# Four-layer graph network on one core: the neighbour product of layer 1 in seven half-size products, the other whole, and three engines queued by hand up to the first expert

## The chip, the core and the metric

The kernel runs on one core of one Trainium2 chip. A core has a TensorE (PE) for matrix products, a VectorE (DVE), a ScalarE (ACT), a GpSimd (POOL) and a SyncE (SP) whose queue issues most transfers from device memory. Engines run side by side and wait for each other by semaphores. Matrix products are written into PSUM, eight banks of 128 x 512 float32; the other engines take them from there. The metric is the device time of one execution in microseconds (us), the median of several runs.

## The reference

512 nodes, 512 features, 16384 edges (src, dst); four layers, each on a normalised, rectified copy of x and added to x. Cut to layers 1 and 2, around which the change stands:

```python
h = jnp.maximum(_layernorm(x, axis=-1), 0.0)
x = x + _L1_gnn_ref(h, ...)
#   alpha = h @ wc;  beta = h @ wn
#   sums = segment_sum(beta[dst], src);  gamma = sums / counts[:, None]
#   return alpha + gamma + bias
h = jnp.maximum(_layernorm(x, axis=-1), 0.0)
x = x + _L2_gnn_ref(h, ...)
#   gates = softmax(h @ gate_W + gate_b), the two largest of four experts
#   each expert, twice: h = relu(aggr(h) @ W_l + b_l + h @ W_r), aggr the mean over neighbours
```

Layer 0 is an attention layer with a feed-forward part and two norms; layer 3 a graph convolution. The tolerance of the output asks for float32 products; sums over neighbours are done with a matrix of edge counts, exact in the faster reduced form (fp32r), so that only the other factor is split into a high and a low part.

## The kernel before

Nodes are tiled in four blocks of 128 (`xs[:, b, :]`, `h[:, b, :]`), and a product over features needs the transposed copy `hT[:, k, nodes]`, which `turn` (L189) makes: four transposes on PE into one bank, one ScalarE copy out. `mm` (L196) is a row of products into one bank. Weights come by `load_w` (L81) into five rotating buffers, on SP's queue; a load waits until the products that read the buffer's last content are done.

**Layer 0's end.** `ff_down` (L427) gives the feed-forward result of block b; `residual` (L379) adds h on DVE; `norm2_a`, `norm2_b`, `norm2_c` (L433 to L445) are the layer's norm, the addition to xs, and the next layer's norm with rectification. A norm's statistics and small steps are on DVE (L145 to L161, L175), its logarithm and exponential (L138, L140) and final scaling (L182) on ScalarE. Up to the product of block 3 the order of PE, DVE and ScalarE is written out by hand (`tc.manual_schedule`, L480); block 3's norm stands after it (L700, L708).

**Layer 1** (L735 to L781). `beta_of` (L742): one block of hT times wns, four products of 128x512, then `split` (L711) on ScalarE (high part) and DVE (low part). `alpha_of` (L747): a bias add on DVE, one block of hT times wcs, an add on DVE. `gamma_of` (L753): the neighbour sum of a block, eight fp32r products of the count matrix CT with both parts of beta, needing all four blocks of beta; then scaling and addition to xs (L756), layer 2's norm with h and its high part hs (L182, L184) on ScalarE, the low part (L758) on DVE. Only PE's order is by hand here (L760): beta 0, transposes 2, beta 1, alpha 0 and 1, transposes 3, beta 2 and 3, alpha 2 and 3, sums 0 to 2, transposes of layer 2's block 0, sum 3, transposes 1. DVE's and ScalarE's orders are set by the scheduler, from priorities and readiness as it models them.

**Layer 2's start** (L781 to L795): per block the gate products (`pg`) and the sums over neighbours of h (`pag`), transposes of blocks 2 and 3 between them.

**Seven half products.** `seven` (L819) does a 512x512 product with seven instead of eight products of halves (Strassen's scheme in Winograd's form): `left_sums` (L799) and `right_sums` (L809) form four sums of quarters of each factor on DVE, `product` (L824) is one half-size product (eight records of 128x256 in the profile), and `plus` (L832) adds a bank to a tile on DVE. Every expert uses it (`hidden` L887, `outer` L937). In `seven` the products come in the order 0, 5, 4, 6, 1, 3, 2; two sums (u2, u3) read bank b between products 5, 6 and 3, which add to the same bank. `XR` (L865, L869) are the right sums of hT and agT for all experts, `weights0` (L872) loads an expert's two first weights and makes their left sums; both `weights0(0)` and `weights0(1)` stand ahead of `hidden(0)`, and the scheduler has put their sums wherever DVE was free, from the feed-forward part on. `gates` (L899) is a row of small DVE instructions.

Of the kernel before, what the change touches and what calls it, by code (L numbers as in the profile page):

```python
# [18 lines left out]
P = 128  # L19
# [17 lines left out]
def fast(  # L37
# [442 lines left out]
    with tc.manual_schedule(engines={ET.PE, ET.DVE, ET.Activation}):  # L480
# [206 lines left out]
        nc.vector.reciprocal(ideg_b, ideg_b)  # L687
        ff_up(1, 4)
# [11 lines left out]
    y23 = residual(p3, 3, "y2")  # L700
# [7 lines left out]
    norm2_c(3, norm2_b(3, *norm2_a(3, y23)))  # L708
    ffp.release()

    def split(hi, lo, full, copy):  # L711

        copy(hi, full)  # L713
        nc.vector.tensor_sub(lo, full, hi.bitcast(F32))
# [3 lines left out]

    ideg = main.tile([P, NB], F32, name="ideg")
    icnt = main.tile([P, NB], F32, name="icnt")  # L720
    nanf = main.tile([P, NB], F32, name="nanf")
    nc.vector.tensor_scalar(ideg, deg[:, :NB], 1.0, None, op0=ALU.max)
    nc.vector.reciprocal(ideg, ideg)
    isd1 = main.tile([P, NB], F32, name="isd1")
    nc.vector.tensor_scalar(isd1, deg[:, :NB], 1.0, None, op0=ALU.add)
    rs4 = rsqrt_end(*rsqrt_begin(isd1, NB, "isd"))
    isd = main.tile([P, NB], F32, name="isd")
    nc.vector.tensor_copy(isd, rs4)
    nc.vector.tensor_scalar(icnt, cnt, 1.0, None, op0=ALU.max)
    nc.vector.reciprocal(icnt, icnt)  # L730
    nc.vector.reciprocal(nanf, cnt)
    nc.vector.tensor_scalar(nanf, nanf, 0.0, None, op0=ALU.mult)


    wcs, wns = load_w(wc, "wcs"), load_w(wn, "wns")  # L735
    bias1_b = load_bc(bias1, "bias1_b")

    pair = main.tile([P, 2, NB, D], F32, tag="pair", name="pair")
    beta = pair.bitcast(R)
    hs = main.tile([P, 2, NB, D], R, tag="hs", name="hs")  # L740

    def beta_of(b):  # L742
        p = bank(f"pbe{b}")
        mm(p, [(blk(hT, k, b), wns[:, k, :]) for k in range(KB)])
        split(beta[:, 0, b, :], beta[:, 1, b, :], p, nc.scalar.copy)

    def alpha_of(b):  # L747
        nc.vector.tensor_add(xs[:, b, :], xs[:, b, :], bias1_b)
        p = bank(f"pal{b}")
        mm(p, [(blk(hT, k, b), wcs[:, k, :]) for k in range(KB)])  # L750
        nc.vector.tensor_add(xs[:, b, :], p, xs[:, b, :])

    def gamma_of(b):  # L753
        p = bank(f"psu{b}")
        mm(p, [(blk(CT, j, b), beta[:, i, j, :]) for j in range(NB) for i in range(2)])
        nc.vector.scalar_tensor_tensor(xs[:, b, :], p, icnt[:, b:b + 1], xs[:, b, :], op0=ALU.mult, op1=ALU.add)  # L756
        norm_relu((b,), "n2_", hs[:, 0, b, :])
        nc.vector.tensor_sub(hs[:, 1, b, :], h[:, b, :], hs[:, 0, b, :].bitcast(F32))  # L758

    with tc.manual_schedule(engines={ET.PE}):  # L760
        beta_of(0)
        turn(hT, h, 2, "h2_")
        beta_of(1)
        alpha_of(0)
        alpha_of(1)
        turn(hT, h, 3, "h2_")
        beta_of(2)
        beta_of(3)
        alpha_of(2)
        alpha_of(3)  # L770
        for b in range(NB - 1):
            gamma_of(b)
        turn(hT, h, 0, "h3_")
        gamma_of(3)
        turn(hT, h, 1, "h3_")

    ct_p.release()
    te_p = ctx.enter_context(tc.tile_pool(name="te_p", bufs=1, side="right", reuse_waits="tile"))


    pg = bank("pg")  # L781
    pag = [bank(f"pag{k}") for k in range(KB)]
    with tc.manual_schedule(engines={ET.PE}):
        for b in range(NB):
            mm(pg[:, b * NX:(b + 1) * NX], [(blk(hT, k, b), gw[:, k, :]) for k in range(KB)])
            for k in range(KB):
                for i in range(2):
                    nc.tensor.matmul(pag[k], blk(hs[:, i, :, :], b, k), C[:, b, :], start=(b == 0 and i == 0),
                                     stop=(b == NB - 1 and i == 1))
            if b < 2:  # L790
                turn(hT, h, b + 2, "h3_")
# [7 lines left out]
    def left_sums(t, s, keep=None):  # L799

        a11, a12, a21, a22 = (quarter(t, j, i) for i in range(2) for j in range(2))
        nc.vector.tensor_add(s[:, 0], a21, a22)
        nc.vector.tensor_sub(s[:, 1], s[:, 0], a11)
        last = a21 if keep is None else keep
        nc.vector.tensor_sub(last, a11, a21)
        nc.vector.tensor_sub(s[:, 2], a12, s[:, 1])
        return a11, a12, s[:, 2], a22, s[:, 0], s[:, 1], last

    def right_sums(t, s, keep=None):  # L809

        b11, b12, b21, b22 = (quarter(t, i, j) for i in range(2) for j in range(2))
        last = b12 if keep is None else keep
        nc.vector.tensor_sub(s[:, 0], b12, b11)
        nc.vector.tensor_sub(s[:, 1], b22, s[:, 0])
        nc.vector.tensor_sub(last, b22, b12)
        nc.vector.tensor_sub(s[:, 2], b21, s[:, 1])
        return b11, b21, b22, s[:, 2], s[:, 0], s[:, 1], last

    def seven(name, terms, first, result):  # L819


        pa, pb, pc = (bank(f"{name}_{i}").rearrange("p (m n) -> p m n", m=2) for i in "abc")

        def product(p, i, some, fresh=False):  # L824
            for m in range(2):
                for l, r in some:
                    for k in range(2):
                        nc.tensor.matmul(p[:, m, :], l[i][:, k, m * P:(m + 1) * P], r[i][:, k, :], start=fresh,  # L828
                                         stop=(k == 1), skip_group_check=True)
                        fresh = False  # L830

        def plus(x, p, y):  # L832
            t = uu.tile([P, 2, W], F32, tag="u", name=f"u_{name}") if y is None else y
            nc.vector.tensor_add(t, p, x)  # L834
            return t
# [16 lines left out]
    ws = ctx.enter_context(tc.tile_pool(name="ws", bufs=4, reuse_waits="tile"))  # L852
    uu = ctx.enter_context(tc.tile_pool(name="uu", bufs=6, reuse_waits="tile"))

    def sums_tile(name):
        return ws.tile([P, 3, 2, W], F32, tag="ws", name=f"ws_{name}")

    def copied(p):
        t = uu.tile([P, 2, W], F32, tag="u", name="u_first")
        nc.scalar.copy(t, p)  # L860
        return t, t

    pair = main.tile([P, 2, NB, D], F32, tag="pair", name="sums")
    sums = pair.rearrange("p g s (k n) -> p g s k n", k=2)
    XR = [right_sums(hT, sums[:, 0, 0:3], sums[:, 0, 3])]  # L865
    agT = main.tile([P, KB, N], F32, tag="agT", name="agT")
    for k in range(KB):
        nc.vector.tensor_mul(agT[:, k, :], pag[k], ideg_b)
    XR.append(right_sums(agT, sums[:, 1, 0:3], sums[:, 1, 3]))  # L869
    eTs = {}  # L870

    def weights0(e):  # L872
        l = []
        for nm, src_w in (("wr0", Wr), ("wl0", Wl)):
            w = load_w(src_w[e, 0], f"{nm}_{e}")
            l.append(left_sums(w, sums_tile(f"{nm}_{e}")))
        return l
# [603 lines left out]
```

## Time and profile before

| | |
|---|---|
| three runs | 522.4, 521.95, 521.9 us; median 521.95 |
| the profiled execution | 522.04 us, its span 520.4 us, mean granted PE clock 0.986 |
| PE busy | 482.4 us, 93% of the span |
| DVE busy | 356.5 us, 68% |
| ACT busy | 155.8 us, 30% |
| POOL busy | 2.8 us |
| layer 1's first product to expert 0's first product, on PE | from 208.40 to 261.24 us |

Times in the profile are microseconds from the span's start. Each row of a timeline gives the start, the length, the engine, the line of the kernel, the operation, what is written from what, shapes, and how many records are merged; a bracket gives the idle time before and what ended it. A float32 product has two records in the trace, an fp32r one has one. The length of a PE row contains the way through the array, so consecutive rows overlap; the time that a group takes of PE is from its start to the next group's. The chain of work that ended last is followed back from the end: at each step to what released it. A table of stretches gives per stretch the busy time of PE, PE's weight loads, DVE, ACT and POOL with the number of instructions, then the clock granted to PE as a share of full speed.

### The profile page before, as it was taken

How to read it: one execution, taken by the hardware profiler on the slowest of the kernel's cores; microseconds unless marked ns; L12 is line 12 of the kernel's file. 1: busy time of each engine (PE TensorE's matmuls, PEld its weight loads, DVE VectorE, ACT ScalarE, POOL GpSimd, SP SyncE). 2: the span in 40 equal slices, each digit the busy share in tenths (PEclk: the TensorE clock that was granted, in tenths of full speed). 3: DMA queues.
4: the chain of work that ended last, by engine and by line, in shares of the span. 5: the costliest groups of instructions: out<-in, count | busy, mean ns of one | idle time of the engine just before them, and what ended most of it. 6: DMA issues, size and time to landing. Idle time of an engine off the chain costs nothing.

```text
span 520.4 us, 5638 instructions
## 1 busy us (share of the span) xinstructions
PE 482.4 (93%) x2159; PEld 358.9 (69%) x2159; DVE 356.5 (68%) x731; ACT 155.8 (30%) x316; POOL 2.8 (1%) x10
## 2 busy tenths in 40 slices
PE   2999889697999999998999999999999999999993
PEld 1798556354774584445888888888888888885552
DVE  8899999998987776928562547831687136656642
ACT  3886344341531231312402131021202121122452
POOL 2000000000000000000000000000000000000000
PEclk9999999979999999999999999999999999999998
DMA  7810201300002133422002141200322040000002
GB/s 253 296 70 1 81 1 48 115 22 0 1 21 66 55 124 119 142 73 90 0 1 91 71 151 37 102 35 20 144 81 81 1 161 1 0 1 1 0 1 85
DMA packets 18497, 34.41 MB, mean 66 GB/s; under 512 B 1528, under 2 KB 2080, under 8 KB 18464
## 3 DMA queue, kind: packets, MB, share of 16 engines
q1 hardware_dynamic: 17504, 32.47, 18.5%
q10 hardware_dynamic: 960, 1.51, 0.8%
q8 instruction: 19, 0.31, 0.3%
q14 instruction: 14, 0.11, 0.1%
HBM read 32.93 MB, written 1.05 MB: 65 GB/s over the span
## 4 chain that ended last, share of the span: by engine, by line
PE 74%; DVE 18%; ACT 3%; issue 2%; DMA 1%; ACTq 0%; DVEq 0%
PE pe_b L828 8%; PE pff L198 5%; PE pe_a L828 5%; PE pf L430 5%; PE pe_c L828 5%; PE pq L198 5%; PE pz_b L828 3%; PE po_b L828 3%; PE pqk L198 3%; PE pwo L377 3%; PE pbe L198 3%; PE ph L198 3%; PE cps L273 2%; DVE m L304 2%; PE pz_c L828 2%; PE po_a L828 2%
## 5 line engine op out<-in xcount | busy, mean ns | idle before, releaser
L834 DVE TENSOR_TENSOR u_pe<-pe_b,u_first 128x512 f32<-128x512 f32 x12 | 8.3, 692 | 55.7 <-PE pe_b L828 55.7
L198 PE MATMUL pq<-zz,C 128*128 128x512 f32 x128 | 32.7, 409 | 0.0
L271 DVE TENSOR_SCALAR ohs<-iota_h,src_f,dw_i 128x256 bf16<-128x256 f16 x104 | 28.8, 340 | 1.7 <-PE cps L273 1.6
L198 PE MATMUL pff<-hT,w 128*128 128x256 f32 x128 | 28.6, 381 | 0.7 <-issue 0.7
L198 PEld LDWEIGHTS pq<-zz,C 128*128 128x128 f32 x128 | 24.1, 189 | 6.6 <-issue 1.2
L273 PE MATMUL cps<-ohs,ohd 128*128 128x256 bf16 x104 | 19.5, 289 | 9.7 <-DVE ohs L271 9.7
L430 PE MATMUL pf<-w,ffT 128*128 128x512 f32 x64 | 28.1, 592 | 0.0
L932 ACT ACTIVATE re<-te,gt 128x512 f32<-128x512 f32 x16 | 11.6, 723 | 54.8 <-DVE te L930 54.8
L894 ACT ACTIVATE eT<-u_pe,vecs 128x256 f32<-128x256 f32 x24 | 10.9, 500 | 56.5 <-DVE u_pe L834 56.5
L198 PEld LDWEIGHTS pff<-hT,w 128*128 128x128 f32 x128 | 24.1, 190 | 5.0 <-issue 1.7
L273 PEld LDWEIGHTS <-ohd 128*128 128x128 f16 x128 | 15.7, 145 | 13.6 <-DVE ohd L266 8.0
L299 PE MATMUL psc<-qT,kT 64*128 64x256 f32 x128 | 17.8, 421 | 4.2 <-DVE s L310 4.2
L430 PEld LDWEIGHTS pf<-w,ffT 128*128 128x128 f32 x64 | 11.9, 190 | 13.9 <-issue 13.9
L304 DVE TENSOR_REDUCE m<-psc 128x256 f32<-128x2048 f32 x8 | 18.3, 2286 | 1.7 <-PE cps L273 1.2
L310 DVE TENSOR_TENSOR s<-psc,m 128x1024 f32<-128x1024 f32 x16 | 18.8, 1215 | 0.1
L713 ACT CAST zz<-u_pz 128x512 fp32r<-128x512 f32 x12 | 7.4, 618 | 37.7 <-DVE u_pz L834 37.7
L299 PEld LDWEIGHTS psc<-qT,kT 64*128 64x128 f32 x128 | 13.2, 204 | 7.8 <-issue 6.5
L348 PE MATMUL aps<-s,v 128*64 128x256 f32 x128 | 15.8, 388 | 3.0 <-DVE nt_l L145 3.0
L338 DVE TENSOR_TENSOR s<-s,r 128x2048 f32<-128x2048 f32 x8 | 18.3, 2286 | 0.1
L311 ACT ACTIVATE s<-s 128x1024 f32<-128x1024 f32 x16 | 16.8, 1054 | 3.3 <-DVE s L310 2.8
L933 DVE TENSOR_TENSOR xs<-xs,re 128x512 f32<-128x512 f32 x16 | 11.0, 690 | 9.3 <-ACT re L932 9.3
L828 PE MATMUL pe_b<-sums,wr 128*128 128x256 f32 x64 | 16.4, 379 | 0.0
(264 smaller groups left out, 1039.9 us busy)
## 6 DMA issues: line engine op xcount, KB each, us to landing
wr<-in_L_gnn_Wr_dram SPq DMA_DIRECT2D x8, 1024.0 KB
wl<-in_L_gnn_Wl_dram SPq DMA_DIRECT2D x8, 1024.0 KB
w<-in_L_gnn_W_dram SPq DMA_DIRECT2D x5, 1024.0 KB
wk<-in_L_gnn_Wk_dram SPq DMA_DIRECT2D x1, 1024.0 KB
wq<-in_L_gnn_Wq_dram ACTq DMA_DIRECT2D x1, 1024.0 KB
wv<-in_L_gnn_Wv_dram SPq DMA_DIRECT2D x1, 1024.0 KB
wo<-in_L_gnn_Wo_dram SPq DMA_DIRECT2D x1, 1024.0 KB
bl_b<-in_L_gnn_bl_dram SPq DMA_DIRECT2D x4, 256.0 KB
```

Source lines behind the costliest of these rows:

```text
L198: nc.tensor.matmul(p, a, c, start=(i == 0), stop=(i == len(pairs) - 1))
L271: nc.vector.tensor_scalar(ohs, iota_h, src_f[:, c:c + 1], dw_f[:, c:c + 1], op0=ALU.is_equal, op1=ALU.mult)
L273: nc.tensor.matmul(cps, ohd[0][:, :, c % 8], ohs, start=(c == 0), stop=(c == NCH - 1))
L299: nc.tensor.matmul(psc[i][:, 4 * g + j, :], kT[o:o + HD, j, b * P:(b + 1) * P], qT[o:o + HD, j, cols], start=True, stop=True)
L304: nc.vector.tensor_reduce(m, psc[i].rearrange("p h n -> p n h"), axis=AX.X, op=ALU.max)
L310: nc.vector.tensor_sub(s[:, g, :], psc[i][:, g, :], m[:, None, :].to_broadcast([P, 4, W]))
L311: nc.scalar.activation(s[:, g, :], s[:, g, :], AF.Exp, scale=1.0 / 8.0)
L338: nc.vector.tensor_mul(s, s, rz[i].to_broadcast([P, H, W]))
L348: nc.tensor.matmul(aps[hf][j // 2][o:o + HD, j % 2, :], v[:, b, (2 * j + g) * HD:(2 * j + g + 1) * HD], s[:, 4 * g + j, :], start=(b == 0 ...
L377: nc.tensor.matmul(p, blk(qT, k, b), wo[:, k, :], start=(k == 0), stop=(k == KB - 1))
L430: nc.tensor.matmul(p, ffT[b // 2][:, f, c:c + P], w2[f // 4][:, f % 4, :], start=(f == 0), stop=(f == FB - 1))
L828: nc.tensor.matmul(p[:, m, :], l[i][:, k, m * P:(m + 1) * P], r[i][:, k, :], start=fresh, stop=(k == 1), skip_group_check=True)
```

## The change

- beta is no longer made by blocks but by the seven half products, in an order of its own (0, 1, 4, 5, 6, 3, 2); `product` and `plus` become functions of their own, and `left_sums` and `right_sums` are taken apart into steps that can be queued one by one. beta's quarters are split as they come (`split_hi` returns the subtraction to be queued later).
- alpha stays whole, and its blocks stand between beta's products: 0, 1, 2 early, 3 last.
- From the last block of the feed-forward part to the sums of agT, PE, DVE and ScalarE are all in one hand-written order, with block 3's norm, expert 0's left sums (`f0`, taken in the gaps), the gates, the neighbour sums and, at the end, expert 1's left sums (`F1 = weights0(1)`).
- In the neighbour sums, each block's add of the next sum stands between the statistics and the small steps of its norm; the gates of a block stand before the next transposes.
- The small tiles of degrees (ideg, icnt, nanf, isd) are made earlier, after the long reciprocal L687, and their two ScalarE instructions stand ahead of the copies of feed-forward groups 4 and 6. The bias adds of layer 1, which the scheduler had put into layer 0's norms, are queued before alpha's adds.

The order after, from the diff (helpers such as `alpha_mm`, `gamma_mm`, `turn_pe` issue PE's part and return the other engine's):

```diff
+    def product(p, i, some, fresh=False):
+        for m in range(2):
+            for l, r in some:
+                for k in range(2):
+                    nc.tensor.matmul(p[:, m, :], l[i][:, k, m * P:(m + 1) * P], r[i][:, k, :], start=fresh,
+                                     stop=(k == 1), skip_group_check=True)
+                    fresh = False
+    def plus(x, p, y=None):
+        t = uu.tile([P, 2, W], F32, tag="u", name="u_sum") if y is None else y
+        nc.vector.tensor_add(t, p, x)
+        return t
...
+    def beta_quarter(i, j, value):
+        return split_hi(*(beta[:, g, 2 * i:2 * i + 2, j * W:(j + 1) * W] for g in range(2)), value)
+    def gamma_begin(b):
+        return norm_relu_begin((b,), "n2_")
+    def gamma_end(b, begun):
+        norm_relu_end((b,), "n2_", begun, hs[:, 0, b, :])
...
-    with tc.manual_schedule(engines={ET.PE}):
-        beta_of(0)
...
+    with tc.manual_schedule(engines={ET.PE, ET.DVE, ET.Activation}):
+        RB, rb = right_steps(wns, sums_tile("wns"))
+        ub, last = (uu.tile([P, 2, W], F32, tag="u", name=n) for n in ("u_first", "u_last"))
+        L, ls = left_steps(hT, sums_tile("hT"), last)
+        B = [(L, RB)]
...
+        ba = halves("pbe_a")
+        product(ba, 0, B, True)
+        nc.scalar.copy(ub, ba)
+        a3 = norm2_a(3, y23)
+        al = alpha_mm(0)
+        turn(hT, h, 2, "h2_")
+        n3 = norm2_b(3, *a3)
+        al1 = alpha_mm(1)
+        norm2_c(3, n3)
+        product(ba, 1, B)
+        lo00 = beta_quarter(0, 0, ba)
+        add_bias1(0)
+        al()
+        rb[0]()
+        al2 = alpha_mm(2)
+        turn(hT, h, 3, "h2_")
+        add_bias1(1)
+        al1()
+        ls[0]()
+        rb[1]()
+        ls[1]()
+        bb, bc_ = halves("pbe_b"), halves("pbe_c")
+        product(bc_, 4, B, True)
+        product(bb, 5, B, True)
+        rb[2]()
+        ls[2]()
+        rb[3]()
+        ls[3]()
+        add_bias1(2)
+        al2()
+        u2 = plus(ub, bb)
+        product(bb, 6, B)
+        lo00()
+        f0[0]()
+        u3 = plus(ub, bb)
+        product(bb, 3, B)
+        lo11 = beta_quarter(1, 1, plus(u3, bc_))
+        product(bc_, 2, B)
+        f0[1]()
+        lo11()
+        lo10 = beta_quarter(1, 0, plus(ub, bb))
+        f0[2]()
+        al3 = alpha_mm(3)
+        lo10()
+        lo01 = beta_quarter(0, 1, plus(u2, bc_))
+        f0[3]()
+        lo01()
+        add_bias1(3)
+        al3()
+        for step in f0[4:6]:
+            step()
...
+        psu = [gamma_mm(b) for b in range(3)]
+        psu[0]()
+        g0 = gamma_begin(0)
+        psu[1]()
+        gamma_end(0, g0)
+        g1 = gamma_begin(1)
+        cp = turn_pe(0)
+        cp()
+        psu.append(gamma_mm(3))
+        psu[2]()
+        gamma_end(1, g1)
+        hs_low(0)
+        gates_mm(0)
+        g2 = gamma_begin(2)
+        cp = turn_pe(1)
+        cp()
+        around_mm(0)
+        psu[3]()
+        gamma_end(2, g2)
+        hs_low(1)
+        gates_mm(1)
+        g3 = gamma_begin(3)
+        cp = turn_pe(2)
+        cp()
+        around_mm(1)
+        f0[6]()
+        gamma_end(3, g3)
+        hs_low(2)
+        cp = turn_pe(3)
+        cp()
+        f0[7]()
+        hs_low(3)
+        gates_mm(2)
+        around_mm(2)
+        gates_mm(3)
+        around_mm(3)
...
+        XR = [right_sums(hT, sums[:, 0, 0:3], sums[:, 0, 3])]
+        for k in range(KB):
+            nc.vector.tensor_mul(agT[:, k, :], pag[k], ideg_b)
+        XR.append(right_sums(agT, sums[:, 1, 0:3], sums[:, 1, 3]))
+        F1 = weights0(1)
```

In `left_steps` the four steps are a21 + a22, the sum less a11, a11 - a21, and a12 less the second; a11 and a12 are the quarters of hT for nodes 0 to 255, a21 and a22 those for nodes 256 to 511. `right_steps` does the like on wns: b12 - b11, b22 less that, b22 - b12, b21 less the second.

## Prediction

> **What bounds the kernel now.** I read the page's engine totals first, then the engine shares of the chain of work that ended last.
>
> ```profile
> PE 482.4 (93%) x2159; PEld 358.9 (69%) x2159; DVE 356.5 (68%) x731; ACT 155.8 (30%) x316; POOL 2.8 (1%) x10
> ...
> PE 74%; DVE 18%; ACT 3%; issue 2%; DMA 1%; ACTq 0%; DVEq 0%
> ```
>
> TensorE (PE) is busy 93% of the span and carries most of the chain: outside its waits, time goes only where PE work goes. So I read the changed stage as PE's own timeline, from the end of the feed-forward part to the first product of expert 0 (columns: start in us, length, engine, line, operation, out<-in, records; the bracket is idle time before it and who ended it).
>
> ```profile
> 208.40 3.60 PE L198 MATMUL pbe<-wns,hT 128*128 128x512 f32 x8
> 211.83 0.60 PE L193 MATMUL tp_h<-ident,h 128*128 128x128 f32 x4
> 212.27 3.60 PE L198 MATMUL pbe<-wns,hT 128*128 128x512 f32 x8
> 215.70 7.03 PE L198 MATMUL pal<-wcs,hT 128*128 128x512 f32 x16
> 222.57 0.60 PE L193 MATMUL tp_h<-ident,h 128*128 128x128 f32 x4
> ...
> 229.88 7.03 PE L198 MATMUL pal<-wcs,hT 128*128 128x512 f32 x16
> 236.34 6.16 PE L198 MATMUL psu<-pair,CT 128*128 128x512 f32 x24
> 244.88 0.66 PE L193 MATMUL tp_h<-ident,h 128*128 128x128 f32 x4 [2.38 <-ACT h L182]
> 245.30 2.87 PE L198 MATMUL psu<-pair,CT 128*128 128x512 f32 x8
> 248.02 1.11 PE L193 MATMUL tp_h<-ident,h 128*128 128x128 f32 x4
> ...
> 252.09 0.60 PE L193 MATMUL tp_h<-ident,h 128*128 128x128 f32 x4
> 252.53 0.95 PE L198 MATMUL pg<-gw,hT 128*128 128x4 f32 x8
> 253.34 2.10 PE L788 MATMUL pag<-C,hs 128*128 128x512 f32 x8
> ...
> 261.24 1.89 PE L828 MATMUL pe_a<-hT,wr 128*128 128x256 f32 x8
> ```
>
> The reader is to see: from 208.40 to 242 PE never waits, so the last norm of layer 0 is hidden already. PE waits once, before the first turned block after the neighbour sums. And the next transposes take 1.11 us where the later ones take 0.60. The table of stretches tells why (last columns: granted clock, DMA share, GB/s):
>
> ```profile
> 242.94:246.35 3.41, 1.47 (x9) 1.29 (x10) 2.71 (x11) 2.24 (x7) 0.00 (x0) 1.00 0.00 0
> 246.35:249.77 3.42, 3.42 (x14) 2.66 (x12) 2.46 (x12) 2.53 (x6) 0.00 (x0) 0.50 0.00 0
> ```
>
> PE was busy for 1.47 of 3.41 us, and in the next 3.42 us its granted clock was 0.50.
>
> **Units for the walk,** from starts of consecutive rows. Whole 128x512 product of a block: 212.27 to 215.70, 3.43. Four transposes: 0.44. One half-size product (eight 128x256 records): 1.72 (pe_a from 261.24, the next group from 262.96). One neighbour sum (psu): from the end of pal's stream, 229.88 + 6.86 = 236.74, three take until 242.33, 1.87 each. Transposes and gates of a block: 252.09 to 253.34, 1.25. Sums around (pag): 1.94. Another engine starts on a PSUM result 0.20 after PE has moved on (pal's add at 222.77 for 222.57). A DVE instruction on 128x512 starts 0.60 after the one before, or 0.73 if it reads that one's result:
>
> ```profile
> 199.05 0.69 DVE L802 TENSOR_TENSOR ws_wr<-wr 128x512 f32<-128x512 f32 x1 [6.19 <-DMA wr<-in_L_gnn_Wr_dram]
> 199.78 0.69 DVE L803 TENSOR_TENSOR ws_wr<-ws_wr,wr 128x512 f32<-128x512 f32 x1
> 200.39 0.68 DVE L805 TENSOR_TENSOR wr<-wr 128x512 f32<-128x512 f32 x1
> ...
> 314.59 0.68 DVE L834 TENSOR_TENSOR u_pz<-pz_b,u_first 128x512 f32<-128x512 f32 x1
> 315.32 1.59 PEld L828 LDWEIGHTS pz_b<-wl,h 128*128 128x128 f32 x8 [0.80 <-DVE u_pz L834]
> 315.32 1.99 PE L828 MATMUL pz_b<-wl,h 128*128 128x256 f32 x8 [0.40 <-DVE u_pz L834]
> ```
>
> The last two rows show what the same seven products cost elsewhere when PE waits for DVE: PE goes 0.73 after DVE's add starts, and its eight records take 1.84 (the next group starts at 317.16), 0.12 more than without a wait.
>
> **The change part by part.**
>
> *1. beta in seven half products.* Eight half-size units (4 x 3.43) become seven: 13.73 - 12.04 = **1.69 us less PE work**, all on the path.
>
> *2. What these seven wait for.* Products 0 and 1 need only nodes 0 to 255, so they, alpha 0 to 2 and both transposes run back to back: 208.40 + 2 x 1.72 + 3 x 3.43 + 2 x 0.44 = 223.01. The norm of block 3 is not late: block 2's took 6.9 us without the bias add (y at 201.73, h done at 209.27, less 0.6), and two new ScalarE copies of 0.6 sit in its queue, so h(3) is there at about 216.7, and its transposes start at 222.57.
> But every other sum needs block 3: ScalarE copies hT 0.20 later (0.59 long), DVE follows 0.03 after that, at 223.83, and PE 0.73 later, at 224.56. **Wait 1.55**, then product 4 (1.84) and 5 (1.72) until 228.12.
> The add of u2 must read bank b before product 6 goes into it, and stands behind nine DVE instructions: four left and three right sums, a bias add, alpha 2's add. Seven steps of 0.60, one of 0.73 (alpha's add reads the biased row), one of 0.60: u2 starts at 229.36, PE at 230.09. **Wait 1.97.**
> Product 6 ends at 231.93. In `seven`, product 1 stands between 6 and 3; here it went ahead, so u3 (at 232.13) holds product 3 until 232.86. **Wait 0.93.** Products 3 and 2 end at 236.42 and alpha 3 covers the last quarter's add, cast and subtraction (done by about 238.9): the sums begin at 239.85 against 236.74.
> With three restarts of 0.12 the added waits are **4.81 us**.
>
> *3. Neighbour sums and gates.* Three sums end at 245.46. In before DVE goes from the first sum's add at 238.80 to PE's transposes at 244.88, 6.08 us, because adds and statistics of blocks 1 and 2 stand within the chain. Queued by hand, only block 1's add does. From the same rows: add to nr 1.80, nr 0.40, add 0.66, four small steps 0.57, ScalarE 0.20 later, PE 0.77 after that: 4.40. The add itself starts at 241.98 (behind two sums of weights, which start at 240.65). Transposes at 246.38: the wait is 0.92 and not 2.55 (244.88 - 242.33), **1.63 less**.
> Then the fourth sum at full clock takes 1.94 (as pag) where 245.30 to 248.02 was 2.72, and gates 0 covers h(1): **0.78 less**. Transposes and gates at half clock took 2.12 (248.02 to 250.14) against 1.25: **0.87 less**, if the clock stays up.
> Walking DVE on (3.33 us from one block's add to the next), h(3) reaches PE at 255.71, when PE has been free since 255.11: **0.60 more**, a wait that before does not have.
>
> *4. What is only moved.* The bias adds leave the norms' chains, where 0.6 each was hidden. The small degree reciprocals go behind the long reciprocal (189.52 to 192.87), and two ScalarE instructions that wait for them now stand ahead of the copy of feed-forward group 4, at 190.54; it moves to about 193.2, but PE reads it only past 198, after four of the eight blocks of the next product: nothing. Expert 0's sums of weights leave 199 to 216 for DVE's gaps; that stretch's cover was PE's 13.73 us of feed-forward. Expert 1's eight sums move behind the sums of agT: from 265.5 they end about 270.6, and u2 of expert 0 is ready at 271.3, PE needs it at 261.65 + 6 x 1.72 = 271.97. It fits by 0.7; each us later costs one. On SP nothing changes places; wl of expert 1 is issued when wns is free (236.6 in place of 230.07) and read at 268; in before it landed 5.5 us after its issue. Nothing.
>
> **Sum:** -1.69 + 4.81 - 1.63 - 0.78 - 0.87 + 0.60 = +0.44. The first product of expert 0 starts 0.4 later, and from there the queues are alike. The profiled execution took 522.04 (span 520.4): **522.5**. The median of the runs shown, 521.95, is 0.09 lower.
>
> **Unknown prices.** Restarts: 0.12 each, or nothing, if the weights are loaded ahead (-0.36). DVE steps: 0.60 or 0.73 each; were all ten up to u2 at 0.73, +1.2. The wait at h(3): none to 0.9 by rounding in the chain, as a like chain is hidden in before (-0.60, +0.3). All four chains together, 0.07 each: 0.3. I take the nearest rows, as above; the ends give 521.2 to 523.7. The clock is priced from its row: nothing, or a stretch of 3.41 us at half speed, at most 1.7.
>
> The trace's row says that 2.55 us without matmuls, nearly all inside one stretch, halved the clock; 2.96 us before 125.14, split over two stretches, left it at 1.00. [...]
>
> **Rivals.**
> *A. The waits themselves halve the clock (slower).* Place: 222.57 to 232.86, three waits of 4.45 us in 10.3. Deciding point: a stretch with PE busy at 1.47 of 3.41 or less. From 228.12 the wait of 1.97 leaves 1.44 of 3.41 if a stretch begins just there; with before's stretches (borders at 222.46, 225.87, 229.28) the busy share stays above half. So it takes an unlucky border. Price 0.8 (as before paid) to 1.7: **524.2** at worst. DVE at its slow spacing (+1.2) leads to the same side.
> *B. The sums do not hold PE (faster).* If DVE were ahead at products 4, 6 and 3, the 4.81 fall away: **517.7**. For it: DVE idles from 219.4 to 223.8. Against: the sums read block 3, which ScalarE delivers at 223.80, and the order of DVE's queue is fixed. Half of it would be 520.1.
> *C. The clock's credit is not won.* A half-clock stretch falls somewhere in this stage after as it did before, and costs the 0.87 again: 523.4. For it: four waits of 0.6 to 2 us in place of one of 2.55. Against: none is as long as the one whose stretch was halved.
>
> **Chances.** The forecast's walk, 521.2 to 523.0: 0.65. A: 0.15. C or slow DVE: 0.10. B, in full or half: 0.10. The range takes in A's worst price, and leaves out B: 521.2 to 524.2. A difference of 0.2% (1.04 us) is about what a measurement of this kernel can tell from none: faster by more 0.10, within 0.67, slower 0.23 (A, and most of C).
>
> **What would show it.** In PE's timeline after: waits of about 1.6, 2.0 and 0.9 before pbe_c, and twice before pbe_b, ended by DVE; psu from about 239.9; a wait of 0.9 before the first tp_h, 0.6 before the last; granted clock 1.00 from 210 to 270; pe_a at 261.7. I am wrong if pbe_b does not wait for u_sum, if a stretch there shows clock 0.50, or if DVE's sums of expert 1 hold u_sum past 272.

## The result and the profile after

| | before | after |
|---|---|---|
| median of 20 executions each | 521.92 us (520.96 to 522.58) | 521.83 us (520.50 to 524.37) |
| ratio after / before | | 1.0002, 95% interval 0.999 to 1.0013 |
| the profiled execution | 522.04, span 520.4 | 524.05, span 522.3 |
| TensorE's first product of layer 1 to expert 0's first product | 52.84 us | 56.27 us |
| from there to TensorE's last matmul | 251.30 us | 251.36 us |
| TensorE's last matmul to the end | 7.85 us | 5.80 us |

The change makes no difference that can be measured, and the forecast, 522.5, said so. But the table already shows that its reasons cannot be whole: the changed stage is longer by 3.4 us in this execution, not 0.4, and the end of the program is shorter by 2.05, of which the forecast says nothing. The profiled execution is one of three of the twenty at 524, with a mean granted clock of 0.983 to 0.986; the other seventeen lie between 520.5 and 522.4, at 0.990 or 0.991, so its timeline has to be read with that in mind.

The same two lines of the page and of the chain as were shown of before:

```profile
PE 483.4 (93%) x2183; PEld 364.4 (70%) x2183; DVE 367.7 (70%) x744; ACT 156.9 (30%) x317; POOL 2.8 (1%) x10
...
PE 73%; DVE 20%; ACT 4%; issue 2%; DMA 0%; DVEq 0%; ACTq 0%
```

VectorE has 11 us more work and two points more of the chain. TensorE's own timeline of the changed stage (columns as in the prediction):

```profile
225.03 1.99 PE L783 MATMUL pbe_c<-ws_wns,ws_hT 128*128 128x256 f32 x8 [1.40 <-DVE ws_hT L749]
...
230.64 3.06 PE L783 MATMUL pbe_b<-wns,u_last 128*128 128x256 f32 x8 [1.89 <-DVE u_sum L789]
234.49 3.78 PE L783 MATMUL pbe_b<-ws_wns,hT 128*128 128x256 f32 x8 [0.78 <-DVE u_sum L789]
...
242.91 6.14 PE L198 MATMUL psu<-pair,CT 128*128 128x512 f32 x24
249.84 0.66 PE L858 MATMUL tp_h<-ident,h 128*128 128x128 f32 x4 [0.78 <-ACT h L182]
...
259.11 0.66 PE L858 MATMUL tp_h<-ident,h 128*128 128x128 f32 x4 [0.48 <-ACT h L182]
...
265.11 1.89 PE L783 MATMUL pe_a<-hT,wr 128*128 128x256 f32 x8
```

The reader is to see five waits, at the five places that the prediction named, each ended by the engine that it named. A bracket counts from the end of the row before, which lies some 0.15 after TensorE has gone on: 1.40, 1.89, 0.78, 0.78 and 0.48 here are 1.55, 2.04, 0.93, 0.93 and 0.63 in the prediction's way of counting, where it had 1.55, 1.97, 0.93, 0.92 and 0.60. But products 6 and 3 take 3.06 and 3.78 instead of 1.99: they run at half clock for the most part. The table of stretches (third column from the right: granted clock):

```profile
228.00:231.41 3.41, 1.52 (x8) 1.02 (x7) 3.31 (x6) 0.00 (x0) 0.00 (x0) 1.00 0.00 0
231.41:234.82 3.41, 2.63 (x7) 1.64 (x6) 1.42 (x3) 0.00 (x0) 0.00 (x0) 0.50 0.00 0
234.82:238.24 3.42, 3.42 (x9) 2.70 (x9) 1.63 (x3) 0.62 (x1) 0.00 (x0) 0.50 0.02 5
```

A stretch border fell at 228.00, and the longest wait (228.75 to 230.64) lies whole in the stretch behind it, so TensorE was busy for 1.52 of 3.41 us; the next two stretches ran at half clock. This is rival A in the flesh, and one of the prediction's own signs of being wrong, a stretch at 0.50 here: with it the neighbour sums begin at 242.91 and not at 239.9, and expert 0 at 265.11 and not at 261.7.

### The profile page after: what moved, and what is told of

Read it like the earlier page. It is cut to its first block, busy times and chain, and to the rows that moved or that the text cites. A ratio compares the mean times of both kernels' runs of the same rounds, so it can differ in the third digit from the quotient of the medians.

```text
span 522.3 us, 5703 instructions
## 1 busy us (share of the span) xinstructions
PE 483.4 (93%) x2183; PEld 364.4 (70%) x2183; DVE 367.7 (70%) x744; ACT 156.9 (30%) x317; POOL 2.8 (1%) x10
## 4 chain that ended last, share of the span: by engine, by line
PE 73%; DVE 20%; ACT 4%; issue 2%; DMA 0%; DVEq 0%; ACTq 0%
PE pe_b L783 8%; PE pff L198 5%; PE pe_a L783 5%; PE pf L430 5%; PE pe_c L783 5%; PE pq L198 5%; PE pz_b L783 3%; PE po_b L783 3%; PE pqk L198 3%; PE pwo L377 3%; PE pal L198 3%; PE ph L198 3%; PE cps L273 2%; DVE m L304 2%; PE po_c L783 2%; PE pz_c L783 2%
## 5 line engine op out<-in xcount | busy, mean ns | idle before, releaser
L789 DVE TENSOR_TENSOR u_sum<-pe_b,u_first 128x512 f32<-128x512 f32 x12 | 8.3, 692 | 50.8 <-PE pe_b L783 50.8
L1002 ACT ACTIVATE eT<-u_sum,vecs 128x256 f32<-128x256 f32 x24 | 10.9, 500 | 52.9 <-DVE u_sum L789 52.9
L726 ACT CAST zz<-u_sum 128x512 fp32r<-128x512 f32 x12 | 7.4, 618 | 37.7 <-DVE u_sum L789 37.7
L789 DVE TENSOR_TENSOR u_sum<-pz_b,u_first 128x512 f32<-128x512 f32 x12 | 8.3, 690 | 11.8 <-PE pz_b L783 11.6
```

## The experiments

Four numbers describe every profiled execution: the stage (first product of layer 1 to expert 0's first product), the half-clock stretches in it, the middle (251.3 to 251.4 us in all thirteen profiles) and the end (TensorE's last matmul to the last instruction). What lies ahead of the stage, 208.2 to 209.4 us, differs from one execution to the next without any change in it (209.39 in b_pad15, 208.56 in b_pad4), so times are compared by medians and stages.

| kernel | median us (runs) | stage us | half-clock stretches in it | end us |
|---|---|---|---|---|
| before, profiled | 521.92 (20) | 52.84 | 1 | 7.85 |
| after, profiled | 521.83 (20) | 56.27 | 2 | 5.80 |
| e1_whole | 520.12 (5) | 50.09 | 0 | 8.02 |
| e3_u2_first | 522.24 (11) | 53.96 | 0 | 5.84 |
| e4_cover | 517.39 (5) | 49.10 | 0 | 5.85 |
| e5_fill | 521.78 (12) | 53.37 | 0 | 6.28 |
| b_pad15 | 519.98 (5) | 52.01 | 0 | 5.64 |
| e1_pad14 | 518.20 (5) | 50.08 | 0 | 5.90 |
| a_pad114 | 523.87 (6) | 53.37 | 0 | 8.44 |
| e2_p1_back | 522.09 (12) | 54.29 | 1 | 5.86 |
| e2_fill | 520.92 (10) | 52.83 | 0 | 6.08 |
| e7_cover2 | 516.61 (4) | 48.49 | 0 | 6.37 |
| b_pad4 | 520.26 (5) | 52.01 | 0 | 6.08 |

In the labels, whole stands for beta in whole blocks, cover for an order that covers every sum, fill for waits filled with matmuls that nobody reads, p1_back for product 1 moved, and pad with a number for so many idle VectorE copies added to before (b), e1_whole (e1) or after (a).

Theory at the outset: the hand-written order gains what the prediction said and the seven products, as queued, cost about as much. Rivals: neither does anything, or the half clock is what decides.

### One part undone: whole blocks in the hand-written order

```diff
-        product(ba, 0, B, True)
-        nc.scalar.copy(ub, ba)
+        pb = [beta_mm(0)]
...
-        bb, bc_ = halves("pbe_b"), halves("pbe_c")
-        product(bc_, 4, B, True)
...
+        pb += [beta_mm(2), beta_mm(3)]
+        lo2, lo3 = beta_hi(2, pb[2]), beta_hi(3, pb[3])
```

> The seven half products of beta are undone: beta is four whole blocks again, in the order of the kernel before on TensorE, VectorE and ScalarE; the hand-written order through the gates and neighbour sums stays. Theory (two parts that cancel): the hand-written order is worth the 1.63 at the first transposes, 0.78 at the next, and some of the 0.87 of clock, less the 0.6 at the last transposes, and the seven products as they are queued cost about as much as that: 1.69 less TensorE work against 4.8 of waits, 3.1. So expert 0 starts 3 us earlier than in the changed kernel and the time is 518.4 to 519.4. Rival 1 (the seven products are worth their TensorE time): taking them away costs 1.7, 523.4. Rival 2 (neither part is worth anything, because the end hangs on something else): 521.8, as both kernels.

Measured: 520.12 (519.31 to 520.57), ratio to before 0.9962, 95% interval 0.9949 to 0.9975. TensorE's timeline:

```profile
208.89 3.60 PE L198 MATMUL pbe<-wns,hT 128*128 128x512 f32 x8
...
243.70 0.66 PE L858 MATMUL tp_h<-ident,h 128*128 128x128 f32 x4 [0.69 <-ACT h L182]
...
252.97 0.66 PE L858 MATMUL tp_h<-ident,h 128*128 128x128 f32 x4 [0.48 <-ACT h L182]
...
258.98 1.89 PE L783 MATMUL pe_a<-hT,wr 128*128 128x256 f32 x8
```

The wait before the first turned block is 0.69 where before had 2.38, and the new one at the last transposes is there. The direction is the theory's and both rivals fall, but the time is 0.7 above the expected band, although the stage, 50.09, is 3.3 shorter than the changed kernel's at full clock (53.37, below), as expected. The missing part is at the other end of the program: 8.02 us from the last matmul to the end, where the changed kernel has 5.80.

### One wait taken down: u2 earlier

```diff
         rb[2]()
         ls[2]()
+        u2 = plus(ub, bb)
+        product(bb, 6, B)
         rb[3]()
         ls[3]()
-        add_bias1(2)
-        al2()
-        u2 = plus(ub, bb)
-        product(bb, 6, B)
...
+        lo00()
+        add_bias1(2)
+        al2()
```

> In the changed kernel the second partial sum u2, for which product 6 waits, is taken ahead of four VectorE instructions that nothing on TensorE needs as early (the fourth right and left sums, one bias add, one add of alpha 2: 4 x 0.69 = 2.8 us), and these come behind it. Theory (VectorE's whole queue is what holds this stage, so a wait that goes comes back later): the wait at product 6 falls from 2.0 to about 0.9, but the low parts of beta come later, new waits stand at the neighbour sums, and expert 0 starts 0.3 to 0.8 later: 522.0 to 522.6. Rival (the single wait is the price): 1.0 to 1.1 goes and stays gone, 520.6.

Measured: 522.24, ratio 1.0003 (0.9994 to 1.0011). In TensorE's timeline:

```profile
229.14 1.99 PE L783 MATMUL pbe_b<-wns,u_last 128*128 128x256 f32 x8 [0.78 <-DVE u_sum L789]
...
239.42 0.50 PE L198 MATMUL psu<-pair,CT 128*128 128x512 f32 x1 [0.35 <-ACT pair L726]
240.15 5.62 PE L198 MATMUL psu<-pair,CT 128*128 128x512 f32 x23 [0.23 <-DVE pair L727]
247.12 0.66 PE L858 MATMUL tp_h<-ident,h 128*128 128x128 f32 x4 [1.35 <-ACT h L182]
```

The wait at product 6 fell from 1.89 to 0.78. Two new ones of 0.35 and 0.23 stand at the neighbour sums, that at the first transposes grew from 0.78 to 1.35, and the stage is 0.6 longer. As expected: here VectorE's whole queue is the limit, and moving one of its instructions ahead moves the wait behind.

### Every sum covered

The order on TensorE becomes 0, alpha 0, transposes, alpha 1, transposes, alpha 2, then 5, 4, 6, 1, 3, 2, alpha 3; VectorE's bias and alpha adds go into its gaps. The core of it:

```diff
+        product(bb, 5, B, True)
+        product(bc_, 4, B, True)
+        al1()
         add_bias1(2)
-        al2()
         u2 = plus(ub, bb)
         product(bb, 6, B)
-        lo00()
+        al2()
         f0[0]()
         u3 = plus(ub, bb)
+        product(ba, 1, B)
+        lo11 = beta_quarter(1, 1, plus(u3, bc_))
```

> Same arithmetic as the changed kernel, another order through beta: after product 0 the alpha products 0, 1 and 2 and the transposes stand on TensorE, while VectorE takes the sums that the products need; then 5, 4, 6, 1, 3, 2 and alpha 3; bias adds and alpha adds are put into VectorE's gaps, so that each partial sum has a product as cover. Theory (the added time is the waits in this stage and nothing else): the waits before products 4, 6 and 3 (1.55, 1.97 and 0.93, summing to 4.45) go but for about 0.45 at the neighbour sums, and the time is 517.3 to 518.4, about 1 below the kernel with whole blocks and about 4 below the changed kernel. Rival 1 (VectorE's work for the seven products, some 20 instructions of 0.69, can't be hidden in this stage in any order): 521 to 522. Rival 2 (the half clock, not the waits, is the price of this stage): about 520.5, the changed kernel at its fastest.

Measured: 517.39, ratio 0.9905 (0.9892 to 0.9917): the theory's band, both rivals fall. In TensorE's timeline one wait is left ahead of the transposes:

```profile
209.20 1.89 PE L783 MATMUL pbe_a<-wns,hT 128*128 128x256 f32 x8
...
236.70 5.61 PE L198 MATMUL psu<-pair,CT 128*128 128x512 f32 x23 [0.23 <-DVE pair L727]
243.03 0.66 PE L858 MATMUL tp_h<-ident,h 128*128 128x128 f32 x4 [0.72 <-ACT h L182]
...
258.31 1.89 PE L783 MATMUL pe_a<-hT,wr 128*128 128x256 f32 x8
```

The same arithmetic in another order is 4.4 us faster than the changed kernel, so the waits were its price and could be avoided.

### The waits filled

```diff
+        def fill(n):
+            for _ in range(n):
+                nc.tensor.matmul(pf[:, :W], hT[:, 0, :P], wns[:, 0, :W], start=True, stop=True)
+
+        fill(3)
         product(bc_, 4, B, True)
...
+        fill(4)
         product(bb, 6, B)
...
+        fill(2)
         product(bb, 3, B)
```

> The changed kernel with nine extra matmuls (128x256, 0.43 each) into a bank that nobody reads: three in the wait before product 4, four before product 6, two before product 3. They should fit in the waits, so no instruction behind them starts later. Theory (the clock is halved when TensorE was busy for less than about half of one of the 3.41 us stretches in which the granted clock is set, and only these waits bring that about here): the profile shows full clock from 221 to 245, and no run of this kernel is above 522.7, where three of twenty of the changed kernel were at 524.1 to 524.4; the middle of the runs stays at 521.6. Rival 1 (idle time as such doesn't halve the clock here; something else makes the runs of 524): runs of 524 stay, or the half clock stands in the profile in spite of the filling. Rival 2 (the extra matmuls delay the products): 522.5 to 525 in all runs.

Measured: 521.78 in the middle of 12 runs, highest 522.21; ratio 0.9996 (0.9987 to 1.0004). In its table of stretches the busy time around the waits is now nearly full and the clock 1.00:

```profile
225.42:228.83 3.41, 3.41 (x18) 3.00 (x17) 3.31 (x7) 0.00 (x0) 0.00 (x0) 1.00 0.03 5
228.83:232.24 3.41, 3.25 (x16) 2.54 (x15) 2.52 (x5) 0.00 (x0) 0.00 (x0) 1.00 0.00 0
```

The extra work costs nothing that can be measured, and no run is at 524. That alone proves little: at 3 in 20, twelve runs without one have a chance of 0.85 to the twelfth, 0.14. But the filled stage is the changed stage at full clock, 53.37 us:

```profile
208.15 1.89 PE L783 MATMUL pbe_a<-wns,hT 128*128 128x256 f32 x8
...
261.52 1.89 PE L783 MATMUL pe_a<-hT,wr 128*128 128x256 f32 x8
```

An execution with nothing filled and the clock up has the same stage (a_pad114, below). The profiled 56.27 less 53.37 gives the price of the two half-clock stretches: **2.90 us**.

### The end of the program

Between VectorE's last arithmetic and the end nothing is computed. VectorE's last row and the span, of before and then of after:

```profile
core 0 of [0], span 520.4 us
...
513.08 0.79 DVE L1007 TENSOR_TENSOR o<-rm,xs 128x256 f32<-128x256 f32 x2 [0.95 <-ACT rm L1006]
```

```profile
core 0 of [0], span 522.3 us
...
517.02 0.79 DVE L1115 TENSOR_TENSOR o<-rm,xs 128x256 f32<-128x256 f32 x2 [0.95 <-ACT rm L1114]
```

From the end of that row: 520.4 - 513.87 = 6.5 us before, 522.3 - 517.81 = 4.5 after. The trace's closing records show where: before, VectorE has a drain at 4.87 us past the last matmul and its next record, a semaphore, at 7.39; after, they stand at 4.74 and 5.07. Whole blocks have the same gap one instruction earlier, counted from the end, and VectorE has one instruction more there (775 records in all against 774; the changed kernel has 789): in both the gap stands ahead of VectorE's 772nd record. That points to a count of instructions. A load of code was the author's guess at a reason, because the profile's page lists two queues that move instructions while the program runs (14 pieces of 8 KB and 19 of 16 KB after). Four kernels moved the count by tiny copies in VectorE's idle time:

```diff
         hidden(2, a2)
+        pad = main.tile([P, 4], F32, name="pad")
+        for _ in range(15):
+            nc.vector.tensor_copy(pad, eTs[1][:, 0, 0:4])
```

> The kernel before with fifteen tiny VectorE copies (128x4) in the idle time of the experts; nothing waits for them. With them VectorE executes as many instructions as in the changed kernel. In the profiles so far the time from TensorE's last matmul to the end is 7.85 us (before) and 8.02 us (whole blocks), with VectorE standing still for 2.4 us on nothing that the trace names, four instructions from its end, and 5.80 to 6.28 us in the four kernels with seven products. Theory (a load of code for VectorE falls due at a fixed count of its instructions; with 14 to 15 more of them the border lies elsewhere, and the changed kernel got 2.0 us from this and from nothing that it computes): the end comes 2.0 earlier, 519.9, though work was added. Rival 1 (the 2 us hang on something else, as the data or the order): 521.9. Rival 2 (the copies cost): above 522.2.

Measured: 519.98, ratio 0.9961 (0.9948 to 0.9974).

```profile
core 0 of [0], span 518.4 us
...
513.33 0.79 DVE L1007 TENSOR_TENSOR o<-rm,xs 128x256 f32<-128x256 f32 x2 [0.95 <-ACT rm L1006]
```

518.4 - 514.12 = 4.3 us: the kernel before with fifteen useless copies more is 2 us faster. Its stage has before's order and, in this execution, full clock throughout:

```profile
209.39 3.60 PE L198 MATMUL pbe<-wns,hT 128*128 128x512 f32 x8
...
245.88 0.66 PE L193 MATMUL tp_h<-ident,h 128*128 128x128 f32 x4 [2.39 <-ACT h L182]
246.29 2.10 PE L198 MATMUL psu<-pair,CT 128*128 128x512 f32 x8
249.01 0.66 PE L193 MATMUL tp_h<-ident,h 128*128 128x128 f32 x4 [0.62 <-ACT h L182]
...
261.40 1.89 PE L828 MATMUL pe_a<-hT,wr 128*128 128x256 f32 x8
```

The same in whole blocks, with `range(14)`:

> Whole blocks with the hand-written order through the gates, and fourteen tiny VectorE copies in the idle time of the experts, so that VectorE executes as many instructions as in the changed kernel. Theory (the border of a code load): 8.02 from the last matmul to the end becomes 5.8 to 6.3, and the time falls from 520.1 to 518.0. Rival (the end does not hang on the count): 520.1.

Measured: 518.20, ratio 0.9926 (0.9914 to 0.9939); 1.92 below the kernel without the copies. And the other way, the changed kernel with 38 copies behind each of three experts:

```diff
         hidden(1, F1)
+        for i in range(0, 38):
+            nc.vector.tensor_copy(pad[:, i % 8, :], eTs[1][:, 0, 0:4])
```

> The changed kernel with 114 tiny VectorE copies, 38 in the idle time of each of three experts: 128 instructions more than whole blocks with the hand-written order, so that the border would lie again where it lies there. Theory: the stall of 2 us at the end comes back, 523.5 to 523.9, where the copies themselves delay nothing (no instruction of TensorE starts later). Rival (the count at the end is not what decides, or loads do not come at multiples of 128): 521.6 to 521.8.

Measured: 523.87, ratio 1.0047 (1.0029 to 1.0065).

```profile
core 0 of [0], span 521.8 us
...
513.91 0.79 DVE L1115 TENSOR_TENSOR o<-rm,xs 128x256 f32<-128x256 f32 x2 [0.94 <-ACT rm L1114]
```

521.8 - 514.70 = 7.1 us; its stage is 53.37, as in the filled kernel, so the copies delayed nothing else. The gap stands ahead of VectorE's 900th record, 128 past the 772nd. One of its six runs is at 526.63; its mean clock, 0.981 against 0.988 and 0.989 in the other five, suggests the changed kernel's half-clock case once more, but it was not the profiled one. The last of this group, the kernel before with `range(4)`:

> The kernel before with four tiny VectorE copies instead of fifteen. Theory (the stall at the end stands between VectorE's fourth and third instruction from the end, so four more move the border ahead of the last branch, where VectorE waits for other things anyway): 7.85 from the last matmul to the end becomes 5.8 to 6.3, 519.9 to 520.2. Rival (the load is waited for wherever its border falls in the last dozen instructions): 521.9, with the 2.4 us of stall four instructions earlier.

Measured: 520.26, ratio 0.9965 (0.9951 to 0.9979), end 6.08. That is just above the band, 1.88 below before measured beside it (522.14): four instructions are enough. VectorE's 772nd record is there the one that reads the flag, ahead of its last branch; it starts 0.92 us past the last matmul, as in the other kernels, and no gap is seen. All four kernels go the theory's way, so the count is shown. That a load of code is behind it is argued: from the last matmul on, the trace has five of the 8 KB pieces in the three kernels with the gap and four in each of the other ten, but it does not say for which engine a piece comes.

### Product 1 back between 6 and 3

```diff
-        product(ba, 1, B)
-        lo00 = beta_quarter(0, 0, ba)
...
         product(bb, 6, B)
-        lo00()
+        product(ba, 1, B)
         f0[0]()
         u3 = plus(ub, bb)
         product(bb, 3, B)
```

> The changed kernel with product 1 back between products 6 and 3, as in the experts' order, so that u3 has a product as cover; its quarter's high and low parts come later on ScalarE and VectorE. Prediction's account (0.93 stands before product 3 because product 1 went ahead): that wait goes. Theory (VectorE's queue): part of it comes back behind, as 0.35 more at the first transposes, so that expert 0 starts 0.6 earlier and the time is 521.1. Rival 1 (a wait that goes is gone): 520.7. Rival 2 (all is given back): 521.7.

Measured: 522.09, ratio 1.0002 (0.9993 to 1.0012): a miss for the theory and for rival 1. Rival 2's 521.7 lies within the interval, but not for its reason: the wait for u3 is gone and that at the first transposes only 0.3 longer,

```profile
247.28 0.66 PE L858 MATMUL tp_h<-ident,h 128*128 128x128 f32 x4 [1.07 <-ACT h L182]
```

while the stretch with the longest wait is followed by one at half clock:

```profile
225.45:228.86 3.41, 1.52 (x7) 1.04 (x6) 3.31 (x6) 0.00 (x0) 0.00 (x0) 1.00 0.00 0
228.86:232.27 3.41, 3.41 (x9) 2.70 (x8) 0.61 (x2) 0.00 (x0) 0.00 (x0) 0.50 0.00 0
```

So the same kernel was run with that idle time filled, `fill(3)` before product 4 and `fill(4)` before product 6 as above:

> Product 1 back between products 6 and 3, as in the run before, and seven extra matmuls (128x256) into a bank that nobody reads, three in the wait before product 4 and four in that before product 6, so that TensorE is not idle there. The run before had a mean clock of 0.986 to 0.989 in all twelve executions (0.990 to 0.991 is usual for the changed kernel), and in its profile one stretch of 3.41 us with 1.53 us of TensorE work was followed by one at half clock inside product 6. Theory (the wait for u3 goes for good except for 0.3 to 0.6, and the half clock took that gain): from the start of the stage to expert 0's first product 52.8 us, against 53.4 in the changed kernel at full clock, and a median of 521.1 to 521.4. Rival (the gain is given back by VectorE, the half clock is not the cause): 522.0 as without the extra matmuls, and no stretch at half clock in either case to tell of.

Measured: 520.92, ratio 0.9976 (0.9967 to 0.9986), stage 52.83. The mean clock is 0.990 to 0.993 in all ten runs, where the twelve without the extra matmuls had 0.986 to 0.989.

```profile
209.21 1.89 PE L783 MATMUL pbe_a<-wns,hT 128*128 128x256 f32 x8
...
246.77 0.65 PE L858 MATMUL tp_h<-ident,h 128*128 128x128 f32 x4 [1.29 <-ACT h L182]
...
262.04 1.89 PE L783 MATMUL pe_a<-hT,wr 128*128 128x256 f32 x8
```

Seven useless matmuls more, 1.2 us less: the stage is as the theory said, the median 0.2 below its band, and the rival falls. The wait's removal is worth 0.54 (53.37 - 52.83), and one half-clock stretch cost 54.29 - 52.83 = 1.46.

### A version that beats both

The edit against e4_cover, around VectorE's sums:

```diff
         al2()
         f0[0]()
+        f0[1]()
         u3 = plus(ub, bb)
...
         lo11()
-        f0[1]()
         lo00 = beta_quarter(0, 0, ba)
...
         al3 = alpha_mm(3)
-        f0[4]()
         lo01 = beta_quarter(0, 1, plus(u2, bc_))
-        f0[5]()
         lo01()
         al3()
+        f0[4]()
+        f0[5]()
```

> The order with every partial sum covered, once more sorted on VectorE: expert 0's left sums are taken where VectorE stood idle (before u3) and after alpha 3's add, and no longer ahead of the last quarter's sum and low part. Theory: the 0.45 before the neighbour sums go (0.23 in the profile's own count), and since that end was set by VectorE, 0.6 in all: 516.8. Rival (the wait only moves to the first transposes, where it stands at 0.7 already): 517.4, as before.

Measured: 516.61, ratio 0.9889 (0.9874 to 0.9905), as the theory said.

```profile
235.12 6.17 PE L198 MATMUL psu<-pair,CT 128*128 128x512 f32 x24
242.04 0.66 PE L858 MATMUL tp_h<-ident,h 128*128 128x128 f32 x4 [0.75 <-ACT h L182]
...
257.31 1.89 PE L783 MATMUL pe_a<-hT,wr 128*128 128x256 f32 x8
```

No wait is left between layer 1's first product and the first transposes; the wait there is 0.75 where e4_cover had 0.72, so the rival falls. This kernel and e4_cover are the only ones in which the seven products beat whole blocks (518.20, without the gap at the end either): by 1.59 here, where their TensorE work is 1.69 less.

## Why the prediction came out right, point by point

Its number held by luck: terms that it got wrong pull in opposite directions, a clock credit of 0.87 that belongs to one execution of the kernel before and 2.0 us at the end of the program that it left out, and with the smaller misses 0.5 is left over. With the count of instructions equal on both sides, the medians separate the parts:

- **The seven products as queued:** after - e1_pad14 = 521.83 - 518.20 = **+3.63**. The prediction's steps 1 and 2 give -1.69 + 4.81 = +3.12; the stage at full clock gives 53.37 - 50.08 = +3.29. Right, wait by wait. The walk as a whole put the changed stage at 52.84 + 0.44 = 53.28; at full clock it is 53.37. The 0.3 between stage and medians is within the intervals.
- **The hand-written order (step 3):** e1_pad14 - b_pad15 = 518.20 - 519.98 = **-1.78**, and by the stage 50.08 - 52.01 = -1.93. The prediction: -1.63 - 0.78 + 0.60 = -1.81. Right. One of its reasons was not: it puts the 0.78 down to a fourth sum at full clock as well as to the cover of h(1) by gates 0. At full clock b_pad15 has the same 2.72 from the fourth sum to the next transposes (246.29 to 249.01), and there TensorE waits for h (0.62 in the bracket) after a sum that ends sooner. So the whole 0.78 is the queue's, and the kernel before waits a second time there, hidden in its profile by the half clock.
- **The clock's credit of 0.87 in step 3: a term that belongs to one execution.** b_pad15 has before's order through the stage and shows it without a half-clock stretch, 52.01 against 52.84. The credit was real against the profiled execution and is no property of the kernel before: of its 54 executions measured beside the experiments, the 28 with a mean clock of 0.988 or less have a median of 522.10, the other 26 one of 521.81, 0.3 apart and not 0.87 (a mean clock does not tell in which stage it was lost). The warning was in the prediction itself, as the "unlucky border" of rival A; it should have been applied to before too.
- **"From there the queues are alike": the step that failed.** The middle is alike to 0.1 us, but the sum closed at expert 0's first product and left the end of the program out, where the changed number of VectorE's instructions took off **2.0** (b_pad15 - before measured beside it, 519.98 - 521.97 = -1.99; a_pad114 - after = +2.04).
- **Sum:** +3.63 - 1.78 - 1.99 = -0.14; measured -0.09. The three are links of one chain of medians, so their sum is no check of them; the stages and a_pad114 are. What the change computes and queues costs 1.9 us (a_pad114 against before), and VectorE's count of instructions gives them back. The predicted reason, parts that cancel to +0.4, is not what happened.
- **Step 4 (moved work at nothing):** the middle is the same in before and after, so the sums of expert 1, which fitted by 0.7, were in time, and so were the rest.
- **Rival A** was right in mechanism and place; its price was mis-sized, 1.7 at most where the profiled execution paid 2.90. The step that failed is "a stretch of 3.41 us": the wait for u3 fell into the first half-clock stretch, TensorE was busy there for only 2.63 of 3.41, and the next stretch stayed at half clock. By time and clock it struck three runs in twenty.
- **Rival B** did not happen in this kernel and is what e4_cover and e7_cover2 made happen: without the 4.81 of waits the stage would be an estimated 53.37 - 4.81 = 48.56, and 49.10 and 48.49 were measured. Its condition "the order of DVE's queue is fixed" held for this change, not for the arithmetic.

On the clock the prediction read that 2.55 us without matmuls in one stretch halved it and that 2.96 us over two did not. After the change a wait of 1.89 us, whole in one stretch, left TensorE busy for 1.52 of its 3.41 us, the next two ran at 0.50, and that cost 2.90 us; so a shorter wait was enough here.

## What to carry to other kernels

When a queue of VectorE feeds TensorE, look for an order in which each partial sum has a product as cover before asking whether fewer products pay: the same instructions cost 3.6 us more than whole blocks in one order and 1.6 less in another. A sum of steps against one profile must include the end of the program, and a term that rests on a half-clock stretch belongs to one execution. Where two kernels differ in their number of instructions, give both the same count with idle copies before crediting 2 us to the change.

## What the runs showed of the hardware

**Which stretch halves the clock.** In before the granted clock changes at 102.99, 109.82, 246.35, 249.77 and 516.01 us, which is 2, 40, 1 and 78 times 3.41 us apart. Over the thirteen profiles, from the first stretch with a clock on record (16 to 19 us in) to 495 us, so without the program's last stretches, take the stretches of 3.41 us at full clock by TensorE's busy time in them: up to 1.29 us, all 17 were followed by one at half clock (1.26 in after at 122.18, 1.17 in e1_pad14 at 122.08); 1.41 to 1.57, three of 7 (1.47 in before at 242.94 was, 1.47 in e2_p1_back at 123.05 was not); 1.64 and more, none of some 1770. A half-clock stretch ended when TensorE was busy throughout (20 of 20, as 3.42 in before at 246.35) and went on at 0.80 to 2.71 of busy time (11 of 11, as 2.63 in after at 231.41). So the stretch ahead of a half-clock one need not be idle: 1.47 to 1.53 us of work in it did not always keep the clock up. The borders do not follow the program: in after one lies 19.16 us past the stage's first product, in a_pad114 they lie 17.64 and 21.05 past it, where no stretch among the same waits has less than 1.99 us of work. So the same waits cost nothing in one execution and 2.90 us in another.

**Instructions are moved while the program runs** (in after past 510 us four pieces of 8 KB and two of 16 KB), and where VectorE's 772nd or 900th record falls behind its last branch, TensorE's last matmul is 7.85, 8.02 and 8.44 us from the end (before, e1_whole, a_pad114), in the other ten kernels 5.64 to 6.37; the medians of the four pairs differ by 1.88 to 2.04. That a border of code lies there is the author's reading and not shown. That it comes back after 128 instructions was assumed ahead of a_pad114; shown is this one return, with 903 VectorE records instead of 775 and the gap at the same instruction.
